# A depthwise 5 x 5 convolution on TensorE: groups of 8 rows and four column phases with two products, in place of 16 rows, two phases and three products

## The chip, the cores and the metric

The kernel runs on one core of one Trainium2 chip. The metric is the device time of the program in microseconds, the median of several executions. A profiled execution gives the times of single instructions and DMA packets.

## What is computed

The reference has two parts, one after the other, on x of shape (4, 128, 128, 128) in float32. The first is a region attention with a convolutional feed-forward part; the second is a pair of quantised 3 x 3 convolutions with batch norms and a residual.

```python
reg = x[:, :, ih, iw]                      # 9 x 9 regions of 16 x 16, step 14
y = _ln(tok, ln1_g, ln1_b); q, k, v = split(y @ w_qkv)
attn = softmax(q k^T / sqrt(32)); tok = (attn v) @ w_out + b_out + tok
merged = overlap-add of the regions / count
y = _ln(xf, ln2_g, ln2_b) @ w_p0 + b_p0    # 128 -> 256 channels
ym = depthwise 5 x 5 convolution, padding 2 # one kernel for each of 256 channels
ym = gelu(gelu(batchnorm(ym)))
y = ym @ w_p2 + b_p2 + xf                  # 256 -> 128 channels
# then: clip to [0, 1], quantise to 4 bits, conv3x3, batchnorm, relu,
#       quantise, conv3x3, batchnorm, + y
```

The change concerns the depthwise convolution and how its input and its result lie in memory.

## The kernel before

**Stages.** The attention stage goes through 36 bands, nine for each of four images (`T = len(bands)`). A band is 16 rows of an image, 14 of them new. In each band nine regions j = 0 to 8 are attended to. `beside(t)` writes out by hand what runs beside the attention in each window j: the first layer norm and the q and k projections of the next band (`ln1_chunks`), the output projection, second layer norm and `w_p0` of the last band (`post_chunks`), and steps of the depthwise conv of an earlier image (`conv_steps`), put into the windows j by the tuple `order`. From band 10 on the conv of the image before runs along; from band 28 on those of the third image and of half of the fourth share eight bands. The other half is done after the last band by `conv_rest`. Then `gelu_stage` and `last_stages` go through 64 units of 8 rows each.

**Order.** PE (TensorE), ACT (ScalarE), DVE (VectorE) and SP (SyncE) are scheduled by hand: each engine runs its instructions in the order in which the program issues them. An instruction that waits holds up all that is behind it on its engine. Nearly all DMAs are issued on SP; those for the conv's halo rows are issued on POOL (GpSimd).

**The depthwise conv before.** An image is cut into groups of GR = 16 rows. Rows of a group and two column phases (even and odd columns) make the contraction: KD = 2 * (16 + 4) = 40 input rows of phases give 16 * 2 = 32 outputs for one channel. The weights are band matrices of 40 x 32, one for each shift s of the phases' columns. Five taps over two phases need three shifts, so there are three products an output (`depthwise`, L672 to L684). A product takes 64 partitions and 32 columns of the array, so that eight channels run side by side: two halves, four quarters q. A tile of the conv has 8 channels and 8 groups of 64 columns, 512 outputs for each partition. ACT copies the result from PSUM to `c` (L743), DVE takes its statistics (L747), and SP stores it to `cv_d`.

**The input of the conv.** In `p0` (in `post_chunks`, L636) a product of four or three rows with `w_p0` goes to PSUM `pm`. ACT adds the bias, splits even and odd columns and writes the tile `y` (L642). There are two tiles `y` for each half h of the channels (`y2t`), used in turn. `store` and `flush` (L502 to L507) issue on SP the DMA from `y` to `y2_d`, in DRAM, at a pitch of 64 columns for each partition, row and phase. `fill` (L686 to L700) loads a tile `u` of the conv from there: the group's own rows on SP, the halo rows on POOL. In bands from 10 on four `p0` steps run in window 8 and the other four in window 0 of the next band.

**The scores.** `scores(j)` (L875) writes two PSUM tiles, `sc0` and `sc1`; the exponentials on ACT (L883) read them. There is one buffer of each, so that the scores of j + 1 wait for the exponentials of j. `values(j)` (L938, L946) runs one window later; DVE takes the reciprocal (L958) and writes `ob` and `part` (L960, L962).

**The late units.** A unit k of the GELU stage is 8 adjacent rows, and its results `cv` come with the two phases of a row one after the other. `second_projection` adds the bias and `xf` in two instructions, one for each phase (L1307). `load_xf` (L209) loads 4 KB for each partition. `conv3x3` (L1243) makes two products of four adjacent rows each.

Of the kernel before, what the change touches and what calls it, by code (L numbers as in the profile page):

```python
# [14 lines left out]
P = 128  # L15
# [16 lines left out]
GR = 16  # L32
CW = P // 2
KD = 2 * (GR + 4)
NCK = 8
NG = P // GR + 1
UW = 4 * NG * CW - CW
# [11 lines left out]
def layers(  # L49
# [41 lines left out]

    y2_d = [dram.tile([4 * GR, P, NG, CW], F32, name=f"y2_d{b}") for b in range(B - 1)]
    y2_d.append(dram.tile([4 * GR, NG, P, CW], F32, name=f"y2_d{B - 1}"))
    cv_d = [dram.tile([P // GR, 2 * P, GR * P], F32, name=f"cv_d{b}") for b in range(B - 1)]
    cv_d.append(dram.tile([2, 2 * P // 4, P // GR // 2, 4, GR * P], F32, name=f"cv_d{B - 1}"))

    dw_d = [
        dram.tile([NCK, 2, 2 * n, 3 * 8 * 32], F32, name=f"dw_d{m}") for m, n in enumerate((2 * GR, KD - 2 * GR))
    ]
    pad_d = dram.tile([2 * GR + 3, 7, 2 * P], F32, name="pad_d")  # L100
    band_d = dram.tile([32, 3, KD, 2 * P], F32, name="band_d")
# [71 lines left out]
    units = [(b, 0, P // GR) for b in range(B - 1)] + [(B - 1, 0, 4), (B - 1, 4, 4)]  # L173
# [36 lines left out]
    def load_xf(n):  # L210
        b, k = pixel_units[n]
        xf = ld[0].tile([P, U], F32, name="xfl")
        nc.sync.dma_start(out=xf, in_=xf_d[b][:, pixels(k)])
        loaded[n].append(xf)
# [6 lines left out]
    with ExitStack() as actx:  # L221
# [17 lines left out]

        y2t = [[y2p.tile([P, RB, 2, CW], F32, name=f"y2_{h}{n}") for n in range(2)] for h in range(2)]  # L240

        ut_ = [up.tile([P, UW], F32, name=f"u{n}") for n in range(3)]
        wt_ = [up.tile([P, 3, 8, 32], F32, name=f"w{n}") for n in range(3)]
# [19 lines left out]
        def band_matrices():  # L263
# [6 lines left out]
            def zeros():  # L270
                zero = scratch(28 * CW)
# [3 lines left out]
                n = (2 * GR + 3) * 7 * 2 * P // P  # L275
# [6 lines left out]
            def edge(b, m, n, g):  # L282
                nc.gpsimd.dma_start(
                    out=rows_in(b, g, m, n), in_=held["zero"][:, : n * CW].rearrange("p (n x) -> p n x", x=CW)
                )
# [8 lines left out]
            def padded_taps():  # L294
                for dy in range(5):
                    nc.sync.dma_start(
                        out=pad_d[GR - 1 + dy, 1:6, :], in_=held["taps"][5 * dy : 5 * dy + 5, :]
                    )

            def by_outputs(ro):  # L300
                for eo in range(2):

                    nc.sync.dma_start(
                        out=band_d[2 * ro + eo].rearrange("s (r e) c -> r s (e c)", e=2),
                        in_=bass.AP(
                            pad_d.tensor,
                            pad_d[GR - 1 - ro, 1 - eo, 0:1].offset,
# [1166 lines left out]
```

## Time and profile before

| What | Value |
|---|---|
| Time, median of 3 runs | 3069.85 us (3060.48 to 3070.08) |
| Profiled execution, its own time | 3066.36 us |
| Its span | 3064.6 us |
| Granted TensorE clock, mean | 0.988 |
| DMA packets | 742035, of which 577969 are under 512 bytes |
| DMA volume, mean rate | 688.21 MB, 225 GB/s |
| Queue of SP (q1), share of 16 engines | 70.6% |
| L680, depthwise products in bands, `pm<-u,w` | 6144 instructions |
| L642, `y<-pm,vectors` | 288 instructions |
| y2 stores on SP | 328 |

A float32 product is two instructions in the profile, so 3072 products of the bands are 6144 instructions. "Busy" is the time in which at least one instruction of a group runs; for matmuls the ends are modelled. A share of DMA is the mean over 16 DMA engines. PEld is the loading of weights, which runs beside the matmuls. Instructions of four columns of the array run side by side, so that a mean duration is longer than the step from one to the next.

### The profile page before, as it was taken

The page shows a single profiled execution, that of the slowest core. Times are in us where ns is not written, and L with a number is a line of the kernel's source. Part 1 is how long each engine was busy: PE and PEld are TensorE (multiplying, and loading weights), DVE is VectorE, ACT ScalarE, POOL GpSimd, SP SyncE. Part 2 cuts the span into 40 slices and gives each one's busy share as a digit, 9 for nine tenths or more (in the row PEclk, how much of TensorE's full clock was granted, in tenths as well). Part 3 has the DMA queues.
Part 4 walks back from the last instruction along what each step waited for, and adds up shares of the span by engine and source line. Part 5 has one row for each costly group of instructions (what it writes and reads, how often), then busy time and mean ns, then how long its engine had stood idle before and what let it go on. Part 6 is the DMA issues. An engine that isn't in the chain of part 4 may idle for free.

```text
span 3064.6 us, 88932 instructions
## 1 busy us (share of the span) xinstructions
PE 2953.6 (96%) x37628; PEld 1425.3 (47%) x37628; DVE 2019.5 (66%) x3181; ACT 1985.5 (65%) x2643; POOL 1023.6 (33%) x1370
## 2 busy tenths in 40 slices
PE   7999999999999999999999999976999999999998
PEld 3545554444444444444444445544444444444443
DVE  4877898777777777776676766744555555666543
ACT  5778787777777777777766767643676776333443
POOL 5444445444443444444344444453111111000000
PEclk9999999999999999999999999988999999999999
DMA  7445776787776677777689888889999997451498
GB/s 163 131 150 175 181 187 180 199 221 219 209 218 189 180 216 212 215 219 203 175 244 246 230 236 227 233 229 278 359 361 357 358 347 246 154 161 53 161 360 304
DMA packets 742035, 688.21 MB, mean 225 GB/s; under 512 B 577969, under 2 KB 616186, under 8 KB 733946
## 3 DMA queue, kind: packets, MB, share of 16 engines
q1 hardware_dynamic: 711258, 648.96, 70.6%
q0 software_dynamic: 12608, 28.74, 3.3%
q10 hardware_dynamic: 17760, 4.71, 0.7%
q8 instruction: 299, 4.90, 0.6%
q14 instruction: 110, 0.90, 0.1%
HBM read 410.68 MB, written 275.51 MB: 224 GB/s over the span
## 4 chain that ended last, share of the span: by engine, by line
PE 83%; DVE 5%; DMA 4%; ACT 4%; issue 3%; SPq 1%; POOL 1%; ACTq 0%; DVEq 0%; POOLq 0%
PE pc L1250 22%; PE pm L513 18%; PE pm L680 9%; PE sc L875 9%; PE po L938 9%; PE pb L1299 7%; PE po L946 4%; PE pm L452 3%; DVE rd L958 2%; DMA y_d<-y 2%; PE sc L680 1%; ACT pt L883 1%; ACT v L866 1%; DVE xn L496 1%; DMA xn<-row 1%
## 5 line engine op out<-in xcount | busy, mean ns | idle before, releaser
L958 DVE RECIPROCAL rd<-po 128x256 f32<-128x256 f32 x324 | 568.6, 1755 | 374.3 <-PE po L946 370.2
L1250 PE MATMUL pc<-q,wq 128*128 128x512 fp8e4 x3168 | 700.6, 381 | 5.0 <-DVE q L1262 5.0
L883 ACT ACTIVATE pt<-sc 128x1024 f32<-128x1024 f32 x648 | 628.4, 1025 | 116.9 <-PE sc L875 58.3
L893 POOL TENSOR_TENSOR sm<-pt 128x512 f32<-128x512 f32 x324 | 414.8, 1280 | 660.8 <-ACT pt L883 467.7
L1250 PEld LDWEIGHTS <-wq 128*128 128x128 fp8e4 x3168 | 309.1, 98 | 406.9 <-issue 44.6
L875 PE MATMUL sc<-q,kr 32*128 32x256 f32 x5184 | 388.6, 402 | 17.3 <-ACT pt L883 16.9
L875 PEld LDWEIGHTS sc<-q,kr 32*128 32x128 f32 x5184 | 241.1, 184 | 268.7 <-issue 179.5
L938 PE MATMUL po<-pt,v 128*32 128x256 f32 x5184 | 350.9, 388 | 13.3 <-DVE part L962 12.7
L680 PE MATMUL pm<-u,w 64*32 64x504 f32 (+3 forms) x6144 | 314.0, 535 | 0.4 <-DVE xf L624 0.4
L893 DVE TENSOR_TENSOR sm<-pt 128x512 f32<-128x512 f32 x324 | 249.4, 770 | 20.4 <-ACT pt L883 20.2
L513 PE MATMUL pm<-xn,wqkv 128*32 128x512 f32 (+1 forms) x2304 | 247.3, 551 | 1.8
L513 PE MATMUL pm<-xn,wp 128*32 128x512 f32 (+1 forms) x2304 | 240.4, 547 | 4.1 <-DVE rstd L459 1.5
L743 ACT COPY c<-pm 128x512 f32<-128x512 f32 x224 | 120.7, 590 | 184.4 <-PE pm L680 175.9
L642 ACT ACTIVATE y<-pm,vectors 128x512 f32<-128x512 f32 (+1 forms) x288 | 182.7, 641 | 86.9 <-PE pm L513 51.5
L1299 PE MATMUL pb<-cv,wp 128*128 128x512 f32 x512 | 232.5, 597 | 4.8 <-ACT cv L1290 4.8
L1258 DVE BATCH_NORM_STATS2 st<-pc 128x6 f32<-128x512 f32 x256 | 165.7, 689 | 85.0 <-PE pc L1250 85.0
L938 PEld LDWEIGHTS po<-pt,v 128*32 128x32 f32 x5184 | 138.3, 109 | 178.2 <-issue 86.3
L946 PE MATMUL po<-sm,ones 128*32 128x256 f32 x2592 | 204.0, 382 | 1.2 <-POOL sm L893 1.1
L965 POOL TENSOR_TENSOR ob<-ob,part 128x32 f32<-128x32 f32 x288 | 128.5, 446 | 218.7 <-DVE part L962 202.4
L747 DVE BATCH_NORM_STATS2 st<-c 128x6 f32<-128x512 f32 (+1 forms) x256 | 146.0, 617 | 83.4 <-ACT c L743 83.3
L1311 POOL TENSOR_SCALAR a<-y 128x1024 f32<-128x1024 f32 x64 | 66.5, 1039 | 392.5 <-DVE y L1307 392.5
L680 PEld LDWEIGHTS pm<-u,w 64*32 64x32 f32 x6144 | 109.8, 106 | 162.8 <-issue 126.3
(172 smaller groups left out, 3721.6 us busy)
## 6 DMA issues: line engine op xcount, KB each, us to landing
cv_d<-c SPq DMA_DIRECT2D x224, 256.0 KB
u<-y_d SPq DMA_DIRECT2D x96, 560.0 KB
cv<-cv_d SPq DMA_DIRECT2D x48, 1024.0 KB
xn<-row SPq DMA_DIRECT2D x76, 512.0 KB
y_d<-y SPq DMA_DIRECT2D x136, 256.0 KB
xfl<-xf_d SPq DMA_DIRECT2D x64, 512.0 KB
id_d<-y SPq DMA_DIRECT2D x64, 512.0 KB
idt<-id_d SPq DMA_DIRECT2D x64, 512.0 KB
```

Of the source, the lines that this page charges most:

```text
L513: nc.tensor.matmul(out[m], w[:, m], v, start=True, stop=True)
L642: nc.scalar.activation(y[:, :n], pm[:, : n * P].rearrange("p (r c e) -> p r e c", r=n, e=2), AF.Identity, bias=bp0[:, h : h + 1],)
L680: nc.tensor.matmul(outs[half][32 * q : 32 * q + 32, j, :, a:z], wt[hs, s, c, :], ut[hs, :, c, a + s - 1 : z + s - 1], start=(s == 1), stop ...
L875: nc.tensor.matmul(sc[h // 2][:, h % 2, kc, :].rearrange("p (r c) -> p r c", c=RS), region(kr, j)[hs, kc * P : (kc + 1) * P], queries(j, h ...
L883: nc.scalar.activation(pt, sc[p], AF.Exp)
L893: add(sm, pt[:, :, 0, :], pt[:, :, 1, :], ALU.add)
L938: nc.tensor.matmul(po[hs, 0, :], v[:, kc, hs], pt[h // 2][:, h % 2, kc, :], start=(kc == 0), stop=(kc == 1),)
L946: nc.tensor.matmul(po[hs, 1, :], ones, sm[h // 2][:, h % 2, :], start=True, stop=True)
L958: nc.vector.reciprocal(rd, po[:, 1, :])
L1250: nc.tensor.matmul(pc[:, h], w[:, t, :], q1[b][:, r + dy : r + dy + RB, dx : dx + P], start=(t == 0), stop=(t == 8),)
L1258: nc.vector.bn_stats(st[:, 2 * n + h, :], pc[:, h])
L1299: nc.tensor.matmul(pb[:, m], wp2[:, h, :], cv[:, h, px], start=(h == 0), stop=(h == 1))
```

## The change

Groups have 8 rows and columns have four phases. The contraction is KD = 4 * (8 + 4) = 48, the outputs are again 8 * 4 = 32, and five taps over four phases need two shifts: two products an output. A channel of an image now has 16 groups of 32 columns, again 512 outputs for each partition.

- Rows of `y2_d` and of the tiles `u` have XW = 33 columns, with one zero column: at the end for phases 0 and 1, at the start for phases 2 and 3. The products of both shifts then have full width, and `y` is written in two instructions, one for each pair of phases.
- Halo rows of a tile `u` take 16 partitions in each half instead of 8 (4 rows of 4 phases instead of 4 rows of 2).
- The order of the 32 outputs is by half of the group (4 rows), phase, row. Results of two adjacent groups are stored together, so that a stored row stays 64 columns long (PAIR).
- A late unit k then holds 4 + 4 rows, 8 rows apart (`first_row`). `load_xf` makes two DMAs, `second_projection` four additions (one for each phase), the last stage two additions, and the output is stored as two runs of four rows.
- The band matrices are built for two shifts: more issues from `pad_d`, fewer pieces to turn.

```diff
-GR = 16
-CW = P // 2
-KD = 2 * (GR + 4)
+GR = 8
+PH = 4
+CW = P // PH
+XW = CW + 1
+KD = PH * (GR + 4)
+PAIR = 2 * GR
...
-UW = 4 * NG * CW - CW
+UW = 4 * NG * XW - XW
...
-    y2_d = [dram.tile([4 * GR, P, NG, CW], F32, name=f"y2_d{b}") for b in range(B - 1)]
+    y2_d = [dram.tile([2 * PH * GR, P, NG, XW], F32, name=f"y2_d{b}") for b in range(B - 1)]
...
-        nc.sync.dma_start(out=xf, in_=xf_d[b][:, pixels(k)])
+        for g in range(2):
+            nc.sync.dma_start(
+                out=xf.rearrange("p (r g n) -> p g r n", g=2, n=P)[:, g],
+                in_=xf_d[b].rearrange("p (g r n) -> p g r n", r=RB, n=P)[:, k // 2 * 4 + 2 * g + k % 2],
+            )
...
-                    nc.scalar.activation(
-                        y[:, :n],
-                        pm[:, : n * P].rearrange("p (r c e) -> p r e c", r=n, e=2),
-                        AF.Identity, bias=bp0[:, h : h + 1],
-                    )
+                    for a in range(2):
+                        nc.scalar.activation(
+                            y[:, :n, 2 * a : 2 * a + 2, a : a + CW],
+                            pm[:, : n * P].rearrange("p (r c e) -> p r e c", r=n, e=PH)[:, :, 2 * a : 2 * a + 2],
+                            AF.Identity, bias=bp0[:, h : h + 1],
+                        )
...
-                                rows_in(b, g, 2 * (GR * h + r0), 2 * (z - a)),
+                                rows_in(b, g, PH * (GR * h + r0), PH * (z - a)),
...
-                for s, (a, z) in ((1, (0, CW)), (0, (1, CW)), (2, (0, CW - 1))):
+                for s in range(2):
...
-                                outs[half][32 * q : 32 * q + 32, j, :, a:z],
-                                wt[hs, s, c, :], ut[hs, :, c, a + s - 1 : z + s - 1],
-                                start=(s == 1), stop=(s == 2),
+                                outs[half][32 * q : 32 * q + 32, j],
+                                wt[hs, s, c, :], ut[hs, :, c, s : s + CW],
+                                start=(s == 0), stop=(s == 1),
...
-                    cv_d[b].tensor, cv_d[b][g0, ch, 0:1].offset, [[CW, P], [2 * P * GR * P, ng], [1, CW]]
+                    cv_d[b].tensor, cv_d[b][g0, ch, 0:1].offset,
+                    [[2 * CW, P], [2 * P * PAIR * P, ng // 2], [1, 2 * CW]],
...
+    def first_row(k, h):
+        return PAIR * (k // 2) + GR * h + RB * (k % 2)
...
-            r = (2 * k + h) * RB
+            r = first_row(k, h)
...
-                for e in range(2):
+                for e in range(PH):
                     nc.vector.scalar_tensor_tensor(
-                        odd_even(y)[:, :, e], pb_[:, :, e, :], bp2, odd_even(xf)[:, :, e], ALU.add, ALU.add
+                        phases(y)[:, e], pb_[:, e], bp2, phases(xf)[:, e], ALU.add, ALU.add
                     )
...
-                nc.vector.tensor_tensor(z, z, idt.pop(at), ALU.add)
+                for g in range(2):
+                    nc.vector.tensor_tensor(z_[:, g], z_[:, g], id_[:, g], ALU.add)
...
-                    out=out[b, :, 2 * RB * k : 2 * RB * (k + 1), :].rearrange("c r w -> c (r w)"), in_=z
+                    out=out[b].rearrange("c (g t r) w -> c g t (r w)", t=2, r=RB)[:, k // 2 * 2 : k // 2 * 2 + 2, k % 2],
+                    in_=z.rearrange("p (g n) -> p g n", g=2),
```

## The prediction

> **What bounds the kernel now.** I read the page first, then busy time by stretches of 64 us, then the groups by form, the timelines of single bands, and the waits.
>
> ```profile
> span 3064.6 us, 88932 instructions
> PE 2953.6 (96%) x37628; PEld 1425.3 (47%) x37628; DVE 2019.5 (66%) x3181; ACT 1985.5 (65%) x2643; POOL 1023.6 (33%) x1370
> ...
> DMA  7445776787776677777689888889999997451498
> ```
>
> TensorE is busy 96% of the span, so shorter matmul work should count. But the DMA row stands at 8 to 9 from slice 20 on. By stage:
>
> ```profile
> core 0: us, PE busy (x) PEld busy (x) DVE busy (x) ACT busy (x) POOL busy (x), PEclk, DMA share, GB/s
> ...
> 256.00:320.00 64.00, 63.43 (x1035) 33.85 (x1024) 49.05 (x75) 51.79 (x79) 28.79 (x37) 1.00 0.59 166
> ...
> 832.00:896.00 64.00, 63.88 (x1065) 30.28 (x1064) 45.30 (x70) 47.26 (x72) 28.92 (x40) 1.00 0.74 208
> ...
> 1600.00:1664.00 64.00, 61.80 (x996) 28.17 (x992) 41.85 (x66) 41.95 (x66) 27.22 (x40) 1.00 0.90 239
> ...
> 2048.00:2112.00 64.00, 42.30 (x1285) 29.80 (x1285) 25.10 (x99) 13.96 (x26) 28.68 (x52) 0.89 0.96 270
> ...
> 2304.00:2368.00 64.00, 64.00 (x229) 28.64 (x228) 35.62 (x54) 44.66 (x35) 9.36 (x9) 1.00 1.00 354
> ```
>
> Bands 10 to 27 (540 to 1500) are bound by TensorE with DMA at 0.74. Bands 28 to 35 already lose 2 us in 64 with DMA at 0.90. The rest of the depthwise conv (2048 on) is bound by DMA: TensorE is idle a third of it. In the GELU stage TensorE is full and DMA has something in flight all the time.
>
> **Removed: a third of the products.** A tile of the conv:
>
> ```profile
> 852.50 2.78 PE L680 MATMUL pm<-u,w 64*32 64x512 f32 x48
> 855.21 1.15 PE L875 MATMUL sc<-q,kr 32*128 32x256 f32 x16
> ```
>
> 48 instructions from 852.50 to 855.21 are 2.71 us; 32 of the same width are 1.81 us. Each tile gives 0.90 us. A band is nine windows j; its tiles lie at j = 1, 3, 5, 7 (in bands 28 to 35 also at 4 and 8). Is TensorE still the bound with 0.90 less? At j = 3 the records show VectorE's `part` done at 866.03 and the matmul that needs it starting at 867.31: 1.28 us of slack, so yes. At j = 7 of band 17, which has no tile, TensorE stalls only 0.6 us with 2.7 us less work. So tiles outside j = 1 give their 0.90 us: 48 in bands 10 to 27 are 43 us, 41 in bands 28 to 35 are 37 us (the narrower tiles of the last image take about the same 2.7 us). What is late next is at j = 1.
>
> **Added: twice the packets of the y2 stores, and twice the activations.** A store of four rows was 128 x 8 packets of 256 bytes; it is 128 x 16 of 132. With 14 rows, two halves h and two phases, 7168 packets a band become 14336. The tile y has two buffers for each h, so the four activations L642 of j = 0 wait for the landing of the four stores of j = 8, about 7 us earlier. This wait is there already:
>
> ```profile
> ACT y L642 <- DMA y_d<-y: 30.6, 34, 3.9
> ```
>
> ```profile
> 1658.24 0.58 ACT L642 ACTIVATE y<-pm,vectors 128x384 f32<-128x384 f32 x1 [3.92 <-DMA y_d<-y]
> ...
> 1660.28 1.94 ACT L883 ACTIVATE pt<-sc 128x1024 f32<-128x1024 f32 x2 [0.61 <-ACT rstd L467]
> ```
>
> ```profile
> 1661.36 0.70 PE L875 MATMUL sc<-q,kr 32*128 32x256 f32 x4 [1.87 <-ACT pt L883]
> ```
>
> ScalarE waited 3.92 us for a store; the exponential behind it was late, and the scores of the next window stalled TensorE 1.87 us. Other bands with waits of 1.5 to 2.0 us lost 0 to 0.4 us: j = 1 forgives about 1.75 us of ScalarE delay, and everything above comes through. If it is late by less, the tile at j = 1 gives up to its 0.90 us too.
>
> How late will the stores be? In band 17/18 the completion records put the four landings at 902.7, 903.6, 904.7 and 905.8, and the activations that need them start at 904.0, 904.9, 905.6 and 906.2. The pace is 1.05 us for 1024 packets. The cost of a packet decides. From the packet records:
>
> ```
> bytes  100  256  768  2048  3072  4096
> ns      13   18   36    84   121   159   (median)
> ```
>
> That is 9 ns and 0.037 ns a byte, so 14 ns for 132 bytes. Packets overlap: the densest 2 us hold 1142 packets of 256 bytes a us, 14 ns each on 16 engines. By these rows 132 bytes need 10 to 11 ns in a dense run. The Trainium skill speaks against it (DMA: Bandwidth & Descriptors, How a descriptor splits into AXI transactions): a transfer that doesn't start on a 256-byte border begins at the border below and pays for the bytes between. A pitch of 132 bytes is nearly never aligned; by its count I estimate 8 to 9 beats of 32 bytes on average, against 8 for an aligned 256, so 14 ns or more. The 100-byte rows are not aligned either and show 13 ns throughout, but they are reads, and only 256. The nearest row to an unaligned write is the 256-byte write, so I take 14 ns; 10.5 is the lower end, 20 the upper. At 14 ns four stores of 2048 need 7.1 us: the fourth lands near 909 instead of 905.8, and with the 0.4 us of slack there ScalarE waits 2.6 us more.
>
> The activations: L642 takes 688 ns at 512 and 583 at 384 elements. The line through both gives 478 and 426 ns for the halves; the square L458 takes 392 and 356 at the same sizes. So a pair costs 0.1 to 0.3 us more than now. At j = 0 and 8 ScalarE has little room; I add 0.4 us to its delay. That is 3.0 us, less 1.75: 1.2 us lost at j = 1. In 16 bands of 10 to 27 that is 19 us, and 4 us more in the two whose j = 1 has no tile. Sum of bands 10 to 27: 43 - 23 = 20 us won. In bands 28 to 35 the wait is 2 to 4 us already, the tile at j = 8 no longer gives the stores its 0.9 us, and the queue is fuller: 3.6 us in each of seven, 25 us, and 3 us for u loads that come late. Sum: 37 - 28 = 9 us won. Bands 0 to 9 have no tiles; their activations of y are spread over three windows and stores have about 6 us to land: 2 us lost (0 to 10).
>
> **u, w and the rest of the conv.** A u tile is 96 partitions instead of 80 of about 8.9 KB: 16 x 420 ns / 16 = 0.4 us of DMA a tile, hidden in bands up to 27. In the rest of the conv nothing hides it: a step loads 320 packets of 2048 bytes now (84 ns) and then 768 of 1056 (48 ns by the line, an estimated 54 if the unaligned start costs); w falls from 80 x 121 to 96 x 84 ns. That is 26.9 thousand ns against 36.9 to 41.5, less 1.6, over 16 engines: 0.5 to 0.8 us a step, 8 to 13 us for 16. Before it TensorE waits 8 us for a chain of the last y stores and u loads; doubled packets add about 4 us. I take 14 us lost (5 to 25). TensorE's four groups there, 83 us together, shrink by 28 us, which buys nothing.
>
> **GELU and last stage.** xfl comes in packets of 512 bytes: 1024 x 27 ns against 128 x 159 ns is 0.45 us of DMA a unit; five transfers of 512 KB at the unloaded 159 ns take 6.4 of the 7.3 us that TensorE needs, so it fits: 3 us lost (0 to 25, all of it if the queue is really the limit). Four additions L1307 of 256 instead of two of 512 add about 0.5 us to VectorE's 4 us a unit, and the 7 us until conv3x3 needs the result hide it. In the last stage 512-element adds and output rows of 2 KB instead of 4 cost VectorE 0.2 us and DMA 0.07 us a unit, beside a full TensorE: 1 us (0 to 6). The other SP issues (92 stores an image instead of 82, 64 xfl loads more) are 0.35 us each on a queue that waits for data.
>
> **Sum:** -20 - 9 + 2 + 14 + 3 + 1 = -9 us. The profiled execution took 3066.4 us around its span of 3064.6; the median of the runs shown is 3.5 us above it. I read the sum against both and say 3060 us; this case's own range is 3040 to 3080. A measurement can tell about 0.3% from no change, 9 us.
>
> **Rivals.**
> *The stores are cheap* (30%): a 132-byte packet needs 10.5 ns. Four stores take 5.4 us, ScalarE's extra delay is 1.2 us with the activations, under the 1.75: j = 1 gives half a tile. Bands 10 to 27 win 50 us, 28 to 35 win 26, the rest loses 12: 3002 us. For it: the straight line of the packet rows. Against it: bands 28 to 35, full already.
> *The stores bound the bands* (30%, slower): partial writes cost 20 ns or more. The skill says under Specifications of the same page that transfers below 512 bytes are read, changed and written back; the 256-byte rows show no sign of it, lying on the line, but no row here has an unaligned write. At 20 ns four stores take 10.2 us, ScalarE's delay is 6 us and j = 1 loses 4.2 us: in 25 bands 105 us and in bands 1 to 9 some 15, against 80 won elsewhere, and 25 lost later: 3130 us. It decides from about 15 ns on, where losses and gains meet.
> *TensorE does not speed up*: runs of 32 columns instead of 64 could stream slower. Against it: 504 columns, unaligned, take 582 ns and 512 aligned 601. It would give 3140; I count it with the slower case.
>
> **How the numbers follow.** Likeliest 40% (about 11 points of it below -0.3%, 17 within, 12 above), cheap 30%, slower 30%. The range holds the cheap case and the slower one to its middle: 2995 to 3130.
>
> **What would show it.** L680 down to 4096 with about 1.8 us a tile in bands; band 16 at 54 to 55 us (56.07 now); the wait of L642 for y_d at 100 us or more instead of 30.6, with scores waiting for `pt` at j = 1; packets of 132 bytes and their time; the rest of the conv longer by 8 us; GELU stage unchanged at 7.3 us a unit. I am wrong if the wait of L642 stays near 30 us (then the cheap case), or if bands 1 to 9, which get no gain, grow too (then the slower).

## The result and the profile after

The changed kernel takes 4028.14 us in the median of 4 runs (4020.4 to 4034.11), the kernel before 3068.97 us beside it: a ratio of 1.313 (95% interval 1.3095 to 1.3169), 959 us slower. The forecast was 3060 us with a range to 3130. The profiled execution has a span of 4032.3 us, and everything below is read from it.

First the span, the busy times and the DMA row:

```profile
span 4032.3 us, 84703 instructions
...
PE 3194.7 (79%) x35068; PEld 1464.8 (36%) x35068; DVE 2081.5 (52%) x3365; ACT 2041.7 (51%) x2931; POOL 1008.4 (25%) x1374
...
DMA  8799999999999999999999999999999999954188
```

TensorE fell from 96% of the span to 79%, while the DMA row went to 9 from the third slice on: before it stood at 4 to 8 in the first half. By stretches of 64 us, a stretch each from bands 0 to 9, 10 to 27, 28 to 35, the end of the conv and the GELU stage:

```profile
core 0: us, PE busy (x) PEld busy (x) DVE busy (x) ACT busy (x) POOL busy (x), PEclk, DMA share, GB/s
256.00:320.00 64.00, 48.53 (x716) 24.58 (x710) 35.64 (x55) 37.24 (x62) 19.80 (x27) 0.90 1.07 120
1184.00:1248.00 64.00, 44.57 (x556) 18.38 (x548) 27.66 (x43) 28.52 (x51) 17.13 (x25) 0.82 1.25 118
2432.00:2496.00 64.00, 50.22 (x688) 22.24 (x672) 29.48 (x45) 35.33 (x60) 18.47 (x27) 0.87 1.14 144
3008.00:3072.00 64.00, 34.92 (x895) 22.37 (x876) 28.94 (x115) 16.63 (x30) 19.98 (x37) 0.76 1.13 323
3200.00:3264.00 64.00, 62.20 (x215) 26.50 (x214) 42.52 (x68) 42.56 (x33) 8.63 (x9) 1.00 1.00 344
```

The last two columns belong together. In the bands the times of the packets add up to 1.07 to 1.25 of the time of all 16 DMA engines (packets of one engine overlap, so that the share can pass 1), and yet they move 118 to 144 GB/s; before, it was 0.59 to 0.90 for 166 to 239 GB/s. They are not moving more, each packet takes longer. The clock granted to TensorE (PEclk) is lower as well, 0.82 to 0.90 in the bands. It is not where the loss begins: e1 below has TensorE's work of before and slower stores, and its mean clock falls from 0.988 to 0.945. But it adds to the loss, as the part on why the prediction was wrong shows. The chain of work that ended last says the same of the stores: y's were 2% of it before, and are 21% now.

```profile
PE 42%; DMA 37%; ACT 8%; DVE 5%; SPq 3%; issue 3%; POOL 1%; ACTq 0%; another core or an unknown queue 0%; DVEq 0%; POOLq 0%
DMA y_d<-y 21%; PE pc L1269 12%; PE pm L526 9%; DMA xn<-row 6%; PE sc L890 5%; DMA row<-rstd 5%; PE pm L694 5%; PE po L953 5%; PE pb L1316 3%; PE po L961 2%; PE pm L465 2%; ACT y L656 2%; ACT cv L1304 1%; DMA id_d<-y 1%; DVE y L1324 1%
```

In the waits (total, times, longest) the activation of y, L642 before and L656 now, waits 673.9 us for its buffer instead of 30.6:

```profile
ACT y L656 <- DMA y_d<-y: 673.9, 141, 21.2
...
DVE xn L509 <- DMA xn<-row: 196.8, 39, 26.7
```

The start of band 16 in the timeline, where the forecast looked for it. The bracket is the idle time of the engine before the instruction and what ended it; SPq is SP's issuing of a DMA:

```profile
1198.26 29.42 SPq L519 DMA_DIRECT2D y_d<-y  x8
...
1198.45 1.94 ACT L898 ACTIVATE pt<-sc 128x1024 f32<-128x1024 f32 x2
...
1207.70 0.74 ACT L656 ACTIVATE y<-pm,vectors 128x192 f32<-128x192 f32 x2 [6.10 <-DMA y_d<-y]
...
1213.51 0.74 ACT L656 ACTIVATE y<-pm,vectors 128x192 f32<-128x192 f32 x2 [5.08 <-DMA y_d<-y]
...
1217.57 0.74 ACT L656 ACTIVATE y<-pm,vectors 128x192 f32<-128x192 f32 x2 [3.33 <-DMA y_d<-y]
...
1223.60 0.74 ACT L656 ACTIVATE y<-pm,vectors 128x192 f32<-128x192 f32 x2 [5.29 <-DMA y_d<-y]
```

Each pair of activations waits for one store to land, 3.3 to 6.1 us, one after the other. And SP itself is held. The durations of the issues between 600 and 1600 us (least, median and most, in ns), first before, then in the changed kernel:

```profile
L506 SPq DMA_DIRECT2D y_d<-y x164: 359/505/3802, 617.5 to 1593.4; - x164
...
L519 SPq DMA_DIRECT2D y_d<-y x124: 370/2798/5903, 625.6 to 1553.2; - x124
```

Later in the same band, where no store is waited for, the products are as fast as the forecast said:

```profile
1272.83 1.95 PE L694 MATMUL pm<-u,w 64*32 64x512 f32 x32
...
1274.71 0.50 PE L890 MATMUL sc<-q,kr 32*128 32x256 f32 x4
```

1.88 us from the tile to the next scores instead of 2.71: the window j = 7 takes 4.40 us, before 5.23. The gain is there; it is buried.

Where the time came from, stage by stage (us, each kernel's profiled execution; bands by the first exponential of each, the GELU stage from its first to its last projection), with the experiments that follow beside it:

```
                      bands 0-9  10-27   28-35  rest of conv  GELU  last
before                    474.0  1014.8  491.0      126.2    462.3  468.1
after                     670.5  1478.4  710.5      194.1    482.1  468.1
e1 260-byte stores        558.8  1216.2  567.8      148.2    462.6  466.6
e2 two of 128 bytes       479.6  1066.5  527.0      134.8    462.6  466.4
e3 two activations        472.8  1018.0  498.2      124.9    462.9  466.2
e5 160-byte stores        497.6  1117.5  626.2      154.4    482.7  467.0
e6 xfl of 512 bytes       476.1  1016.3  499.7      132.3    462.7  467.2
e7 four additions         473.4  1015.6  497.6      125.7    485.1  467.2
e9 two of three products  471.5   975.5  489.6      120.9    461.7  468.8
```

Bands 0 to 9 hold no conv tile at all and are 196 us longer. Whatever it is comes with the stores of y, with the activations that write it, or with the band matrices, which are built there with more issues than before.

The packet records (ns) name the suspect: before, packets of 256 bytes, y's 262144 among them, took 17.8 in the mean; y's 524288 of 132 bytes take 53.9 in the mean, but 14 in the median. The median is the 14 ns of the forecast to the digit. The other end is not: one in ten takes 127 or more.

### The profile page after: what moved, and what is told of

Its sections match the earlier page's. It is cut to its first block, busy times and chain, and to the rows that moved or that the text cites. A ratio compares the mean times of both kernels' runs of the same rounds, so it can differ in the third digit from the quotient of the medians.

```text
span 4032.3 us, 84703 instructions
## 1 busy us (share of the span) xinstructions
PE 3194.7 (79%) x35068; PEld 1464.8 (36%) x35068; DVE 2081.5 (52%) x3365; ACT 2041.7 (51%) x2931; POOL 1008.4 (25%) x1374
## 4 chain that ended last, share of the span: by engine, by line
PE 42%; DMA 37%; ACT 8%; DVE 5%; SPq 3%; issue 3%; POOL 1%; ACTq 0%; another core or an unknown queue 0%; DVEq 0%; POOLq 0%
DMA y_d<-y 21%; PE pc L1269 12%; PE pm L526 9%; DMA xn<-row 6%; PE sc L890 5%; DMA row<-rstd 5%; PE pm L694 5%; PE po L953 5%; PE pb L1316 3%; PE po L961 2%; PE pm L465 2%; ACT y L656 2%; ACT cv L1304 1%; DMA id_d<-y 1%; DVE y L1324 1%
## 5 line engine op out<-in xcount | busy, mean ns | idle before, releaser
L890 PE MATMUL sc<-q,kr 32*128 32x256 f32 x5184 | 479.4, 459 | 160.9 <-ACT pt L898 160.6
L656 ACT ACTIVATE y<-pm,vectors 128x256 f32<-128x256 f32 (+1 forms) x576 | 229.6, 451 | 706.1 <-DMA y_d<-y 673.9
L694 PE MATMUL pm<-u,w 64*32 64x512 f32 (+1 forms) x4096 | 331.0, 646 | 184.3 <-ACT y L656 101.4
L890 PEld LDWEIGHTS sc<-q,kr 32*128 32x128 f32 x5184 | 289.1, 212 | 484.4 <-ACT pt L898 265.9
L953 PE MATMUL po<-pt,v 128*32 128x256 f32 x5184 | 403.8, 435 | 47.1 <-DVE part L977 42.6
L526 PE MATMUL pm<-xn,wp 128*32 128x512 f32 (+1 forms) x2304 | 259.9, 573 | 156.2 <-ACT y L656 153.7
L1316 PE MATMUL pb<-cv,wp 128*128 128x512 f32 x512 | 235.3, 602 | 17.3 <-ACT cv L1307 17.3
L694 PEld LDWEIGHTS pm<-u,w 64*32 64x32 f32 x4096 | 82.7, 116 | 360.7 <-ACT y L656 137.2
L1324 DVE SCALAR_TENSOR_TENSOR y<-pb,vectors,xfl 128x256 f32<-128x256 f32 x256 | 155.8, 679 | 95.0 <-PE pb L1316 95.0
L526 PE MATMUL pm<-wqkv,yr 128*32 128x128 f32 x5184 | 188.4, 286 | 1.3 <-issue 1.3
L509 DVE TENSOR_TENSOR xn<-xn,xt 128x384 f32<-128x384 f32 (+1 forms) x140 | 84.9, 648 | 195.9 <-DMA xn<-row 195.9
```

The source lines that it names most:

```text
L526: nc.tensor.matmul(out[m], w[:, m], v, start=True, stop=True)
L656: nc.scalar.activation(y[:, :n, 2 * a : 2 * a + 2, a : a + CW], pm[:, : n * P].rearrange("p (r c e) -> p r e c", r=n, e=PH)[:, :, 2 * a : ...
L694: nc.tensor.matmul(outs[half][32 * q : 32 * q + 32, j], wt[hs, s, c, :], ut[hs, :, c, s : s + CW], start=(s == 0), stop=(s == 1),)
L890: nc.tensor.matmul(sc[h // 2][:, h % 2, kc, :].rearrange("p (r c) -> p r c", c=RS), region(kr, j)[hs, kc * P : (kc + 1) * P], queries(j, h ...
L953: nc.tensor.matmul(po[hs, 0, :], v[:, kc, hs], pt[h // 2][:, h % 2, kc, :], start=(kc == 0), stop=(kc == 1),)
L1316: nc.tensor.matmul(pb[:, m], wp2[:, h, :], cv[:, h, px], start=(h == 0), stop=(h == 1))
```

## The experiments

Theory 1: the *place* of a write decides. A packet of 132 bytes at a pitch of 132 begins and ends inside some unit of DRAM, and such writes cost several times an aligned one. Theory 2: the *number* of packets decides. Theory 3: the pair of activations does.

### Place against number, with the kernel before (e1, e2, e3)

e1_b65 puts y's packets on rows of 65 columns instead of 64. They are 4 bytes longer for it, and the rows of the tiles u grow with them; the main lines are:

```diff
+XW = CW + 1
-    y2_d = [dram.tile([4 * GR, P, NG, CW], F32, name=f"y2_d{b}") for b in range(B - 1)]
+    y2_d = [dram.tile([4 * GR, P, NG, XW], F32, name=f"y2_d{b}") for b in range(B - 1)]
...
-        y2t = [[y2p.tile([P, RB, 2, CW], F32, name=f"y2_{h}{n}") for n in range(2)] for h in range(2)]
+        y2t = [[y2p.tile([P, RB, 2, XW], F32, name=f"y2_{h}{n}") for n in range(2)] for h in range(2)]
...
```

> The kernel before with rows of 65 columns instead of 64 in the copy of y: the same 7168 store packets a band, each 260 bytes long and 260 bytes from the next, so that nearly none begins or ends on a border of 32 bytes. Theory 1 (the place of a write decides: small writes that begin or end inside a memory line cost several times an aligned one): the mean of a store packet rises from 17.8 to 40 ns or more, the wait of the y activations for y_d from 30 us to some hundreds, and the time is 3300 to 3900 us. Theory 2 (the number of packets decides, wherever they lie): packets stay near 18 ns, the time is 3070 to 3100 us.

Measured: 3451.16 us, ratio 1.125 (1.1215 to 1.1282). The same number of packets costs 382 us more; their mean is 46.5 ns. TensorE's products are those of before. Its wait:

```profile
ACT y L645 <- DMA y_d<-y: 293.0, 119, 8.5
```

e2_bhalf doubles the number, with packets of half the size, and keeps every packet on a border of 128 bytes:

```diff
-                            store(
-                                rows_in(b, g, 2 * (GR * h + r0), 2 * (z - a)),
-                                y[:, a:z].rearrange("p r e x -> p (r e) x"),
-                            )
+                            for c0 in (0, CW // 2):
+                                store(
+                                    rows_in(b, g, 2 * (GR * h + r0), 2 * (z - a))[:, :, c0 : c0 + CW // 2],
+                                    y[:, a:z, :, c0 : c0 + CW // 2].rearrange("p r e x -> p (r e) x"),
+                                )
```

> The kernel before with every store of y cut in two by columns: 14336 packets a band as in the changed kernel, but 128 bytes each and on borders of 128 bytes; TensorE's work as before. Theory 1 (place): packets of 14 ns or less, the wait for y_d below 150 us, the time 3070 to 3130 us. Theory 2 (number): packets near 54 ns in the mean as in the changed kernel, a wait of 500 us or more, the time 3700 to 4000 us and more, since no product is saved.

Measured: 3178.18 us, 1.035 (1.033 to 1.0379), packets of 13.6 ns in the mean, the wait in between:

```profile
ACT y L642 <- DMA y_d<-y: 105.1, 72, 5.3
```

As many packets as in the changed kernel, and 109 us lost instead of 959. That is above the 3070 to 3130 that theory 1 expected: the number is not free either. This kernel also issues twice the DMAs; what of the 109 us is theirs was not separated.

e3_bact writes y in two activations of half the size and stores it as before:

```diff
-                    nc.scalar.activation(
-                        y[:, :n],
-                        pm[:, : n * P].rearrange("p (r c e) -> p r e c", r=n, e=2),
+                    for a in range(2):
+                        nc.scalar.activation(
+                            y[:, :n, a : a + 1],
+                            pm[:, : n * P].rearrange("p (r c e) -> p r e c", r=n, e=2)[:, :, a : a + 1],
```

> The kernel before with the activation that writes y made as two of half the size, stores unchanged. If the pair of activations carries a real part of the loss (theory 3: ScalarE is late at j = 0, not the stores), the time is above 3200 us. If it is only the 0.1 to 0.3 us a pair of the forecast, 3065 to 3110 us.

Measured: 3073.96 us, 1.0013 (1.0004 to 1.0023). Theory 3 falls. A pair takes 223.4 us / 288 = 0.78 us, one activation 0.64 in the mean: the 0.1 to 0.3 us of the forecast.

### The price of a packet by itself (e4)

e4_packets leaves the computation out and runs stores alone, eight of 2048 packets to a group, once each (the branch for the groups of loads is left out here):

```
for t in range(8):
    at = off + t % 2 * 16 * P * pitch + t // 2 * slot
    view = bass.AP(d.tensor, d[at : at + 1].offset, [[pitch, P], [P * pitch, 16], [1, n]])
    s = src[:, : 16 * n].rearrange("p (r x) -> p r x", x=n)
    nc.sync.dma_start(out=view, in_=s)
```

> Leaves all of the computation out: only groups of eight stores of 2048 packets each from SBUF to DRAM, one group after the other, with packet size and pitch changed from group to group, and two groups of loads. Theory 1 (place): 256 bytes at a pitch of 2304 takes about 14 ns a packet on the 16 queues together counted (some 0.9 us a 1024); 132 bytes at a pitch of 2244 takes 50 ns or more; 260 at 2340 and 256 at 2308 are as slow; 128 bytes at 2176 or 2304 takes 14 ns or less; loads of 132 bytes at 2244 take 14 ns. Theory 2 (number): all groups of one count take the same time within a fifth, whatever the place. Which of 132 at 2304 (begins on a border, ends inside one), 144, 160 and 192 bytes at their own pitch is cheap says what border matters: 160 cheap means 32 bytes, 192 alone cheap means 64.

The price is the time of a group, from its first packet's start to its last one's end, by 16384 packets, times 16 engines. So it counts what the engines can do together:

```
bytes  from one partition to the next  begins / ends on 32 bytes   ns a packet
 32    2304                            yes / yes                   10.6
 64    2304                            yes / yes                   11.2
128    2304 (2176 the same)            yes / yes                   11.5
160    2720                            yes / yes                   17.3
192    3264                            yes / yes                   16.1
192    3264, begun 32 bytes later      yes / yes                   18.9
256    2304                            yes / yes                   19.2
512    4608                            yes / yes                   29.0
132    2304                            yes / no                    22.5
144    2448                            one of the two, in turn     27.1
132    2244 (the changed kernel)       mostly no / mostly no       39.6
132    132                             mostly no / mostly no       40.1
128    2244                            mostly no / mostly no       40.4
256    2308                            mostly no / mostly no       42.4
260    2340 (e1)                       mostly no / mostly no       49.4
512    4612                            mostly no / mostly no       48.0
132    2244, read instead of written   mostly no / mostly no       14.4
256    2304, read instead of written   yes / yes                   19.2
```

The trace's own list of issues (number of DMAs, KB of one, median us to landing) mixes groups of one size, but shows the same: 264 KB are the three groups of 132-byte stores, 256 KB the three of 128 bytes, two of which lie on the border, and the last row is 132 bytes read:

```profile
d_w_n_slot_pitch_off<-src SPq DMA_DIRECT2D x24, 264.0 KB, 14.8
d_w_n_slot_pitch_off<-src SPq DMA_DIRECT2D x24, 256.0 KB, 5.0
...
rd<-d_r_n_slot_pitch_off SPq DMA_DIRECT2D x8, 264.0 KB, 5.9
```

Theory 1 holds, and the border is 32 bytes: packets of 160 bytes are as cheap as those of 192, and 192 begun 32 bytes later are still cheap. One open end costs 10 to 11 ns (22.5 against 11.5 for 128 bytes, 27.1 against 17.3 for 160), two cost 19 to 30, at every size from 128 to 512 bytes. In the group of 132 bytes at 2304 no two packets meet in one unit of 32 bytes, so an open end costs without a neighbour too. Reads show no such price: 14.4 ns for 132 bytes off the border, 19.2 for 256 on it. The Trainium skill has this rule (Collectives: The Full Stack, Rules for kernel authors): buffers aligned to 32 bytes, since the hardware otherwise reads, modifies and writes back. It is given there for collectives; here it holds for plain stores. These runs show the border and the price, not what the memory does inside. The rule that the forecast weighed, that everything below 512 bytes is read and written back (DMA: Bandwidth & Descriptors, Specifications), does not show in these prices: aligned packets of 32 to 128 bytes take 11 ns, and 512 bytes off the border pay 19 ns more than on it.

### The change with aligned rows (e5)

If the border is the cause, the changed kernel with rows of 40 columns, 160 bytes, must get most of the time back.

```diff
-XW = CW + 1
+XW = 40
+YW = CW + 1
...
-                                y[:, a:z].rearrange("p r e x -> p (r e) x"),
+                                bass.AP(
+                                    y.tensor, y[:, a * PH * YW :].offset,
+                                    [y.ap[0], [YW, PH * (z - a)], [1, XW]],
+                                ),
...
-        wt_ = [up.tile([P, 2, 8, 32], F32, name=f"w{n}") for n in range(3)]
+        wt_ = [up.tile([P, 2, 8, 32], F32, name=f"w{n}") for n in range(2)]
...
-                    cv = pool.tile([P, 2, ng // 2, 2 * CW], F32, name="cr", bufs=7)
+                    cv = pool.tile([P, 2, ng // 2, 2 * CW], F32, name="cr", bufs=4)
```

> The changed kernel with rows of 40 columns in the copy of y: as many store packets as the changed kernel, 160 bytes long and 160 bytes apart, so that every one begins and ends on a border of 32 bytes (the columns that pad the row are never multiplied). To have room, w keeps two buffers instead of three in the bands, and the results of the rest of the conv four instead of seven. Alone, such packets took 17.3 ns on 16 queues against 39.6 for 132 bytes at their pitch. Theory 1 (place): most of the 960 us goes. 14336 packets of 17.3 ns are 15.5 us of the 16 engines a band against 8.6 in the kernel before; three quarters of the 6.9 us more, less the 0.9 us a tile, and 20 us each in the rest of the conv and the GELU stage give about 3200 us (3100 to 3330). Theory 2 (number of packets, or the pair of activations): 3900 us or more, as the changed kernel.

With two buffers of `w`, tiles of the last image's bands are multiplied by the taps of the tile two later, and wait for those; the amount of work is the same. Measured: 3379.09 us, 1.099 (1.0967 to 1.1018), above the range that I gave and 649 us below the changed kernel. Bands 0 to 27, which have none of those waits, are 534 us shorter than in the changed kernel. Bands 0 to 9 are 23.6 us over before with the band matrices built as in the changed kernel, so these are not the cause. The waits show y's stores relieved, and in bands 28 to 35 a stall that the missing buffer made:

```profile
ACT y L659 <- DMA y_d<-y: 172.0, 97, 4.6
...
PE pm L702 <- DMA w<-dw_d: 77.1, 12, 8.7
```

Without those 77 us it would be near 3300, an estimate. Theory 2 falls as the main cause. The rest of this kernel's loss I put down to the number of packets after all, to longer rows of `u`, and to 20 us in the GELU stage; the first two were not separated.

### The 20 us of the GELU stage (e6, e7)

```diff
-        nc.sync.dma_start(out=xf, in_=xf_d[b][:, pixels(k)])
+        for g in range(2):
+            nc.sync.dma_start(
+                out=xf.rearrange("p (r g n) -> p g r n", g=2, n=P)[:, g],
+                in_=xf_d[b][:, pixels(k)].rearrange("p (r g n) -> p g r n", g=2, n=P)[:, g],
+            )
```

> The kernel before with xfl loaded in two transfers of every other row, packets of 512 bytes instead of 4 KB, as in the changed kernel. If the queue is the reason of the 20 us that the GELU stage of the changed kernel is longer, this stage takes 475 to 482 us instead of 462 and the time is 3080 to 3090 us. If it is VectorE's four additions, the stage stays at 462 to 465 us.

```diff
+                fourth = lambda t: t.rearrange("p (n i k e) -> p k e n i", e=2, k=2, i=P // 4)
+                pb_ = pb_.rearrange("p r e (i k) -> p k e r i", k=2)
                 for e in range(2):
-                    nc.vector.scalar_tensor_tensor(
-                        odd_even(y)[:, :, e], pb_[:, :, e, :], bp2, odd_even(xf)[:, :, e], ALU.add, ALU.add
-                    )
+                    for k_ in range(2):
+                        nc.vector.scalar_tensor_tensor(
+                            fourth(y)[:, k_, e], pb_[:, k_, e], bp2, fourth(xf)[:, k_, e], ALU.add, ALU.add
+                        )
```

> The kernel before with the addition of xfl made in four instructions of 256 elements instead of two of 512, writing every fourth element; transfers unchanged. If VectorE is the reason of the 20 us, the GELU stage takes 475 to 482 us; if the queue is, it stays at 462 to 465 us and the time within 0.3% of before.

e6: 3079.93 us, 1.0016 (1.0008 to 1.0024), GELU stage 462.7 us as before. e7: 3094.51 us, 1.0061 (1.0039 to 1.0082), GELU stage 485.1. So it is VectorE, and not the transfers that I had put my 3 us on. Such an addition of 256 elements is hardly cheaper than one of 512 before (behind the shape: the number of instructions, busy us, mean ns):

```profile
L1307 DVE SCALAR_TENSOR_TENSOR y<-pb,vectors,xfl 128x512 f32<-128x512 f32 x128 | 90.3, 747 | 138.9 <-PE pb L1299 122.7 <-DMA xfl<-xf_d 15.0 <-DMA id_d<-y 1.2
...
L1310 DVE SCALAR_TENSOR_TENSOR y<-pb,vectors,xfl 128x256 f32<-128x256 f32 x256 | 155.8, 680 | 97.1 <-PE pb L1299 95.5 <-DMA xfl<-xf_d 1.5
```

That is no price of 256 elements as such: the same operation on 256 elements at L459 takes 414 ns before. These read `xfl` and write `y` at every fourth element; whether that makes the difference was not tested. Four at 680 less two at 747 are 1.23 us a unit, not 0.5, and that VectorE is idle a third of the stage (42.52 us busy in the stretch of 64 above) does not hide them. The timeline of one unit of e7 shows the ring:

```profile
2419.90 2.43 DVE L1310 SCALAR_TENSOR_TENSOR y<-pb,vectors,xfl 128x256 f32<-128x256 f32 x4 [1.51 <-PE pb L1299]
...
2421.79 1.91 ACT L1290 ACTIVATE cv<-cv 128x2048 f32<-128x2048 f32 x1
...
2422.42 1.04 POOL L1314 TENSOR_SCALAR a<-y 128x1024 f32<-128x1024 f32 x1 [6.68 <-DVE y L1310]
...
2423.49 0.69 DVE L1320 TENSOR_SCALAR a<-a 128x1024 f32<-128x1024 f32 x1 [1.16 <-POOL a L1314]
2423.75 0.30 PEld L1299 LDWEIGHTS pb<-cv,wp 128*128 128x128 f32 x2 [0.48 <-ACT cv L1290]
...
2424.22 0.70 DVE L1262 TENSOR_SCALAR q<-a 128x1024 fp8e4<-128x1024 f32 x1
...
2424.83 1.29 DVE L1258 BATCH_NORM_STATS2 st<-pc 128x6 f32<-128x512 f32 x2
...
2426.20 1.01 ACT L1326 COPY c<-pc 128x1024 f32<-128x1024 f32 x1 [2.50 <-DVE st L1258]
```

VectorE's additions, GpSimd's clamp, VectorE's two steps and its statistics come first; then ScalarE copies `c`, and only behind that copy, in its own order, it prepares the next `cv`, for which TensorE waits. 22.8 us of stage over 64 units is 0.36 us each: the slack of this ring was about 0.9 us, far from the 7 us that I had taken from conv3x3 alone.

### Stores and loads together, and another queue (e8, e10, e11)

e8_mixed leaves the computation out and puts eight loads of 512 packets of 4 KB between the eight stores, once each.

> Leaves all of the computation out: groups of eight stores of 2048 packets, alone and with eight loads of 512 packets of 4 KB between them, on the same queue or the stores on ScalarE's. Alone the loads should take about 40 us (512 packets of 159 ns on 16 engines are 5.1 us each), and the 132-byte stores 40 us as measured. If an engine that sends a store inside a memory line is held for that time, loads and stores together take the sum, 80 us, on one queue or on two. If only the store waits and the engine goes on, they take 40 to 50 us. With 128-byte stores on borders (11.8 us alone) the sum is 52 us.

```
stores           queue of stores  stores alone  loads alone  sum   together
132 at 2244      same as loads    47.4          43.6          91.0  111.4
132 at 2244      another          48.1          43.6          91.7   87.6
128 at 2176      same             11.8          43.6          55.4   72.4
160 at 2720      same             17.7 (e4)     43.6          61.3   74.5
256 at 2304      same             19.6          43.6          63.2   75.0
```

In us. Stores and loads share the engines: off-border stores on a queue of their own, beside the loads, still take nearly the sum. On one queue every mixture is 12 to 20 us above the sum. That suggested to issue y's stores from ScalarE:

```diff
-                            store(
+                            nc.scalar.dma_start(
                                 rows_in(b, g, PH * (GR * h + r0), PH * (z - a)),
```

e10 does it with the kernel before, e11 with the changed one.

> The kernel before with the stores of y issued by ScalarE on its own queue, right behind the activation, instead of SP's list. Stores and 4 KB loads on one queue took 75 us where 63 was the sum of both alone; 132-byte stores on a second queue took 88 against 111. If sharing the queue is part of what y's stores cost, bands 28 to 35 lose their waits and the time is 3040 to 3060 us; against it stands ScalarE's time for the issues, about 8 a band at 0.05 to 0.35 us, which would give 3080 to 3150 us. I have no strong view.

> The changed kernel with the stores of y issued by ScalarE on its own queue. If the price of a packet on the 16 engines is the cause, the time stays above 3800 us, since the engines are the same (88 us against a sum of 91 in the mixed groups). If the shared queue is (stores in front of loads that others wait for), the time falls to 3500 us or below.

Both are slower: 3183.36 us, 1.036 (1.034 to 1.0381), and 4308.28 us, 1.403 (1.3995 to 1.4067). Moving the stores away does not pay. What the shared queue by itself costs these kernels stays open, since ScalarE now pays for the issues: in e10 0.37 us in the median, some nine times a band (328 in 36 bands), in front of the exponentials. In e11 the wait has changed its name only; ScalarE sits in its own issues, which are 17% of the chain (ACTq L665), instead of SP:

```profile
ACT y L656 <- issue: 432.9, 69, 12.5
...
ACT y L656 <- DMA y_d<-y: 83.0, 26, 5.8
```

### The gain alone (e9)

```diff
-                for s, (a, z) in ((1, (0, CW)), (0, (1, CW)), (2, (0, CW - 1))):
+                for s, (a, z) in ((1, (0, CW)), (0, (1, CW))):
...
-                                start=(s == 1), stop=(s == 2),
+                                start=(s == 1), stop=(s == 0),
```

> The kernel before with the third of the three products of a conv tile left out (so the taps of one neighbouring column pair are missing from the conv), nothing else changed: the gain of the change alone. The forecast's first step says 0.90 us a tile on the path: 43 us in bands 10 to 27, 37 us in 28 to 35, so about 2990 us with the rest of the conv unmoved (its 28 us buy nothing, DMA bound). If scores or VectorE are next in line at once, bands 10 to 27 win less than 20 us and the time is above 3030 us.

Measured: 3021.35 us, 0.982 (0.9802 to 0.9843). Bands 10 to 27 win 39 us, as the first step said (43), but bands 28 to 35 win 1.4 us instead of 37. Stretches of bands 10 to 27 and 28 to 35:

```profile
832.00:896.00 64.00, 62.66 (x1004) 30.07 (x1000) 45.99 (x72) 49.28 (x76) 28.55 (x39) 1.00 0.80 219
1600.00:1664.00 64.00, 59.55 (x916) 27.88 (x912) 42.52 (x65) 42.77 (x67) 26.54 (x38) 0.95 0.89 239
```

In the second TensorE works 59.55 us of 64 where it worked 61.80, at the same 239 GB/s: most of what it saves there it idles. So 48 us, the difference of the spans (54 by the medians beside each other), is the whole gain to be had with stores as cheap as before.

## Why the prediction was wrong

**The step that failed is the price of a packet**: "The nearest row to an unaligned write is the 256-byte write, so I take 14 ns; 10.5 is the lower end, 20 the upper." It is 39.6 ns by e4, twice the upper end. The row was near in size and far in what counted: the 256-byte stores of before all lie on the 32-byte border, and the 100-byte reads, which I set against the skill's rule, say nothing of writes. The count of beats (8 to 9 against 8) has no term for a write's open ends, which cost more than the bytes. I had named partial writes as the mechanism of the slower rival, and priced them at 20 ns from rows that could not bound it. Its sign, bands 1 to 9 growing too, came true.

**What that price makes.** A band's packets take 14336 x 39.6 / 16 = 35.5 us of the engines, before 7168 x 19.2 / 16 = 8.6: 26.9 us more. Against e9, which has the gain without the stores, bands 10 to 27 are 27.9 us longer each, and 28 to 35 are 27.6. Bands 0 to 9, with DMA at 0.59 before, are 19.6 longer than before. That 27.9 meets 26.9 so closely is in part luck: with the price of the same stores in e8 (47.4 us a group) it would be 32.9. And the windows say that it isn't one term (by the first exponential of each; us, mean of bands 11 to 26):

```
window j                      0     1     2      3     4   5 to 8    sum
e9                         8.93  3.52  5.65   5.00  8.40    22.48  53.97
changed kernel            26.94  3.53  8.70  10.36  9.83    22.67  82.02
of it at half clock       13.29  3.53  4.08   4.79  1.61     0     27.31
```

Columns as above: the windows 0 to 4, one by one, and 5 to 8 together of band 16 in the changed kernel, a part of its window 3, bands 10 to 27 of the changed kernel, and bands 10 to 27 of e9:

```profile
1198.45:1225.80 27.35, 14.08 (x168) 5.13 (x160) 6.19 (x8) 6.56 (x15) 3.47 (x5) 0.80 1.60 69
1225.80:1229.32 3.52, 2.44 (x16) 1.70 (x16) 1.54 (x3) 3.52 (x6) 2.25 (x3) 0.50 1.78 50
1229.32:1236.80 7.48, 7.48 (x112) 3.61 (x112) 3.96 (x8) 3.70 (x7) 1.52 (x2) 0.83 1.42 69
1236.80:1250.02 13.22, 8.14 (x76) 2.67 (x72) 6.66 (x10) 4.08 (x6) 4.49 (x6) 0.70 0.90 227
1250.02:1260.28 10.26, 10.26 (x140) 4.56 (x140) 5.64 (x10) 6.40 (x10) 2.82 (x4) 0.88 0.74 218
1260.28:1282.90 22.62, 22.56 (x368) 10.70 (x364) 16.50 (x26) 18.77 (x31) 9.14 (x12) 1.00 0.77 212
...
1244.27:1247.87 3.60, 3.60 (x28) 0.65 (x28) 3.57 (x6) 0.59 (x1) 2.38 (x4) 0.50 0.78 172
...
699.10:2177.50 1478.40, 1146.99 (x15176) 508.28 (x15172) 729.75 (x1120) 770.63 (x1267) 438.26 (x608) 0.83 1.11 146
...
500.50:1476.00 975.50, 955.30 (x15176) 459.62 (x15172) 723.21 (x1121) 741.29 (x1121) 445.42 (x607) 1.00 0.77 213
```

Inside window 3, products of a conv tile:

```profile
1244.27 3.63 PE L694 MATMUL pm<-u,w 64*32 64x512 f32 x24 [5.08 <-DVE xf L637]
```

In windows 0 to 2 the stores fill the engines (shares of 1.42 to 1.78 at 50 to 69 GB/s; in e4 a group of such stores alone has 1.48); 21 of the 28 us are lost there. The other 7 are lost in windows 3 and 4, where the engines are not full: TensorE waits for `xf`, which VectorE makes only after its wait for the late row of statistics, and TensorE runs slower. After the stall its clock was granted at 0.50 for a while, and 24 of the products above then took 3.63 us, where 32 took 1.95 in window 7 at full clock. Over bands 10 to 27 TensorE is busy 1147 us for as many instructions as e9 has in 955. In windows 1 to 4, behind the long wait, that is an estimated 5 us a band of TensorE's time (27.4 against 22.0). I had no term for it; how much of it lies on the path was not separated from the waits.

**The wait at j = 0** was the right place, but not the only one. My formula with 39.6 ns gives 2048 x 39.6 / 16 = 5.07 us a store, 20.3 for four instead of 7.1, so 3.0 + 13.2 - 1.75 = 14.4 us a band. Measured are 18.7 (673.9 / 36) for y, close to the 18.0 by which window 0 grew, and 5.5 for the row of statistics (196.8 / 36), which the forecast did not have: it costed the stores by who waits for them, not by what stands behind them. More than two buffers of `y` would tell how much is the wait for the buffer and how much the engines; no run has them.

**The gain.** 0.83 to 0.90 us a tile holds, and so does the sum for bands 10 to 27. For 28 to 35 it fails, by e9. I had read "DMA at 0.90" there and taken 28 us off, but as the price of the stores and not as a limit that was there already. That DMA is this limit is argued from its share, not shown.

**The rest of the conv** lost 68 us instead of 14. Aligned rows (e5) leave 28 of it, so I put some 40 down to the stores still in flight; e5 also has fewer buffers there. **GELU** lost 20 us where I said 3 with an upper end of 25; the size is in my range, the cause was the one I had called hidden. **The last stage** is unchanged (468.1 both; 1 us said). **The pair of activations** is right, by e3. *TensorE does not speed up* falls: 1.88 us a tile.

**The account**, in us against before: e9's gain -48; number of packets and wider rows 259 (e5 against e9, without the GELU stage and the 77 us of `w`); the price of the border 735 (changed kernel against e5, the 77 added back); VectorE in GELU 20. The sum is 966 of the 968 us between the two spans, and must be, since the terms are differences of the same spans. The border's 735 hold all that follows from its stores, the slower TensorE included. The 259 hold the extra padding of e5 too; that the whole 77 us lay on e5's path is taken for granted. No version tried beats the kernel before except e9, which is not the reference's conv.

## What to carry to other kernels

Before a row in DRAM grows by an odd few bytes, look at where its writes begin and end: a store off the 32-byte border costs 40 to 50 ns a packet here from 128 to 512 bytes, and reads tell nothing about it. When no row of the trace shows an operation in the state that the change will have it, the nearest row by size is no bound; leave the upper end open, or multiply it by the packets and see what the whole stage would be. A stage with its DMA engines at 0.9 gave back 1.4 us of the 37 that were forecast for shorter work on TensorE (e9). And a stall can cost more than its wait: here TensorE's granted clock was at half behind it.

## What the runs showed that I had not expected

- The median of the slow packets was exactly that of the fast line (14 ns); the cost lay in the mean (53.9) and the upper tenth (127). Read the mean of packet records.
- The issues of the stores hold SP as well: 2.8 us in the median instead of 0.5. Slow packets alone don't do it: in e1 the median is 0.46 us. With twice the packets to a store it is 1.4 us in e5, where they are cheap, and 2.8 where they are slow.
- Stores and loads that alternate on one queue take 12 to 20 us more than the sum of both alone (72.4 against 55.4 for 128-byte stores). On two queues, with the 132-byte stores, they do not.
- The same group of 132-byte stores took 40.5 us in e4 and 47.4 in e8: its price is not sharp, unlike that of the 128-byte stores (11.83 and 11.82).
